# Conv-attention hybrid on one core: tokens' and feed-forward's PSUM banks in one pool, attention's fixed tiles in other memory, an earlier weighted sum, halved totals

## The chip, the cores and the metric

The kernel runs on one core of one Trainium2 chip, in fp32. The metric is the device time of one launch in microseconds (us), the median of several runs. The engines are called by the names that the profile uses: PE is TensorE's matmuls and PEld its weight loads, DVE is VectorE, ACT is ScalarE, POOL is GpSimd, SP starts the transfers. SBUF is the memory on the chip; PSUM holds the results of matmuls, in eight banks of 128 partitions by 512 fp32 elements.

## What is computed

The input has four images of 128 channels and 64 x 64 = 4096 positions. Each goes through a convolutional attention over positions, then, as 4096 tokens of 128, through a self-attention with 16 heads of 8 and a small feed-forward, and last through a recurrence over tokens.

```python
# layer 0, x: [4, 128, 4096]; conv1x1 is W @ x with a prelu
e1, e2, asm = conv1x1(gn(x), w1), conv1x1(gn(x), w2), conv1x1(gn(x), wa)
score = softmax(einsum('nci,ncj->nij', e1, e2), axis=2)      # 4096 x 4096 per image
x = x + einsum('nij,ncj->nci', score, asm)
# layer 1, t: tokens of 128 = 16 heads x 8
q = qz_ring(heads(ln(t)) + rx_theta)                         # products of cosines
attn = softmax(q @ q^T / sqrt(8))                            # queries, keys and values are q
x1 = ln(ln(t) + concat(attn @ q) @ w_comb^T)
h = relu((cos(x1[..., :8]) * cos(ry_theta)) @ w1^T)
t = t + ln(x1 + h @ w2^T)
# last layer: Wx = batchnorm(ln(t) @ W^T), then
y = sigmoid(Wx[:, step] + y @ V)                             # one step after the other
x = from_tokens(t + ys)
```

Since queries and keys are the same q, the scores are symmetric: a tile of exponentials serves once as it is and once transposed.

## The kernel before

**Stages.** A loop over the four images opens, for each, a convolution stage (`first_stage`, L1352) and an attention stage (`second_stage`, L1400). After the last image come its feed-forward alone (`third_stage`) and the recurrence. Each stage has its own pools of SBUF tiles and PSUM banks; they are given as a name with a shape and a number of buffers, and a tile asked for by `get(name, ...)` takes the next buffer of its pool in turn. A tile whose memory was another's before waits for the last reader of the other. The order of the instructions on PE, ACT and DVE is the order in which the program is written (`manual_schedule`); in the attention stage that holds for POOL as well. In time, image 0's convolution stage runs from 24 to 407 us, its attention to 1659, the convolution stage of image 1 to 2118, its attention to 3375, and so on.

**Convolution stage.** For eight blocks of 512 queries (ic) the inner loop goes over sixteen pairs of key tiles (jp), two pairs a turn: `scores` (L503, two matmuls for each of two key tiles, into a PSUM pair), the exponential to SBUF (L507, ACT), and `weigh` (L514, PE) for the pairs of the turn before, which also adds the exponentials on DVE into a `total` of 128 x 2 x 512. `pieces` are the parts of the three 1x1 convolutions of later blocks, put between; the first of them are wanted by the first turns. After each weighted pair `meanwhile` takes one step of this image's `tokens` (generators that stop at each `yield`, L604) and of the *previous* image's `feed_forwards` (L1305, each `feed_forward`, L1119). The tokens of a block: px, the input transposed on PE and copied to SBUF by ACT (L612 to L614); sum, the totals summed over partitions by matmuls with ones (L619 to L630) in four column groups, transposed on DVE (L632) and inverted; pt, the transposed weighted sum (L640); their combination on DVE (L645), normalisation, cosines, and pq, the transposed q (L688), which is written out as the rows that attention's loads read. The eighth group is the tail: the stage runs it to its combination, and the attention stage steps it to its end between its own units.

PSUM in this stage: one bank `ps_acc`, two pairs `ps_pair`, two single banks `ps_one` (feed-forward: pc, pw, pl, pz, ph, pf, pwx and the convolution's pieces) and one `ps_tok` (px, sum, pt, pq, and the norm's small sums).

**Attention stage.** Eight pairs of heads, for each four blocks b of 512 queries x 2 heads; a block has 20, 20, 16 and 16 units, a unit being two key tiles. Written out, a unit is: its scores (L1012, four matmuls into two PSUM pairs of three), their exponentials (L1024, two instructions on ACT, or four if a unit is split: `off` and two different tiles), the weighted sums of the unit two before (L863, four matmuls with the fixed tile q_aug), and some mirror steps (L842): the products with the transposed exponentials, sixteen steps to a group of four units, four matmuls each. An *off* unit hands its exponentials to DVE for the transposing (L829); an *own* unit, whose tiles both lie in the block's own keys, has no such work. How many mirror steps a unit does is set by a credit, and only if a group is due:

```python
rates = (3.3, 3.0) if b < NQB // 2 else (3.15, 3.0)      # off, own
if end_of_all and not off:
    rates = (0, 4.5)
credit = min(credit + rates[0 if off else 1], 4.75)
...
credit -= run_pending(turn, int(credit))
```

`end_of_all` is the last block of an image. A group's last step adds its bank into `later` on DVE (L856).

**Fixed tiles.** `fixed_tiles` (L725) makes q_aug0 and mirror0 at the start, q_aug1 and mirror1 some turns later: POOL fills them (L728, L733), then copies q into them (`prepare`, L745; `mirror_weights`, L799), which the first weighted sums and the first mirror steps wait for. Their place in SBUF follows the order in which the stage's pools are opened (`fixed`, then `exps`), over what the convolution stage left there.

Of the kernel before, what the change touches and what calls it, by code (L numbers as in the profile page):

```python
# [13 lines left out]
ALU = mybir.AluOpType  # L14
# [12 lines left out]
def kernel(  # L27
# [341 lines left out]
    def layer0(n, xs, xh, norm, shifted, begin, meanwhile):  # L369
# [122 lines left out]
        def scores(ic, jp):  # L492

            if shifted and jp == 0:
                halves(ic)
            s = pair_psum(f"s{n}_{ic}_{jp}")
            hl = state["halves", ic].bitcast(F32R)
            for j in range(2):
                parts = [(e2.bitcast(F32R)[:, ts(2 * jp + j, P)], hl[:, y, :]) for y in range(2)]
                if shifted:  # L500
                    parts.append((ones.bitcast(F32R), state["less", ic].bitcast(F32R)))
                for y, (stationary, moving) in enumerate(parts):
                    nc.tensor.matmul(  # L503
                        s[:, j, :], stationary, moving, start=y == 0, stop=y == len(parts) - 1
                    )
            p = mid_tile(f"p{n}_{ic}_{jp}")
            nc.scalar.activation(p, s, AF.Exp)  # L507
            return p
# [36 lines left out]
        for ic in range(NIC):  # L545
            for jp in range(0, NP, 2):
                if jp == NP // 2 and ic < NIC - 1 and not shifted:
                    halves(ic + 1)
                fresh = [(ic, j, scores(ic, j)) for j in (jp, jp + 1)]
                for i in range(2):  # L550
                    if before:
                        weigh(*before[i])
                        if before[i][1] == NP - 1:
                            take(before[i][0])
                            begin(before[i][0], state)
                    if pieces and i == 0:
                        pieces.pop(0)()

                    meanwhile(2 if ic == NIC - 1 else 1)
                before = fresh  # L560
# [43 lines left out]
    def tokens(im, i, sums):  # L604

        n, q, cols = im["n"], im["q"], ts(i, IC)
        last = i == NTG - 1
        yield  # L610

        pt = transposed(blocks(im["xs"][:, cols]), f"px{n}_{i}", "ps_tok")  # L612
        x0 = im["xs"][:, cols] if last else get("thalf", f"x0_{n}_{i}")
        nc.scalar.copy(x0, pt)  # L614
        yield


        total, taken = sums.pop(i), sums.pop(("sum", i))
        ps = get("ps_tok", f"sum{n}_{i}")[:, 0:P]  # L619
        tv = total.rearrange("p j (k c r) -> p j c k r", c=4, r=32)  # L620
        for j in range(2):
            for c in range(4):
                nc.tensor.matmul(
                    ps[ts(c, 32), :],
                    ones[:, 0:32],
                    tv[:, j, c],
                    start=j == 0,
                    stop=j == 1,
                    skip_group_check=True,
                )  # L630
        by_token = once.tile([P, P], F32, tag="sums", name=f"sums{n}_{i}")
        nc.vector.transpose(by_token, ps)  # L632
        if n == "r":
            inv = stats.tile([P, TG], F32, tag="inverse", name=f"inv{n}_{i}")
        else:
            inv = inverses[:, n * NIC + i, :]
        nc.vector.reciprocal(inv, by_token.rearrange("p (k r) -> p k r", k=TG)[:, :, 0])
        if not last:
            yield
        pt = transposed(blocks(taken), f"pt{n}_{i}", "ps_tok")  # L640
        if not last:
            yield
        for k in range(TG):
            at = ts(k, P)
            nc.vector.scalar_tensor_tensor(  # L645
                x0[:, at], pt[:, at], inv[:, k : k + 1], x0[:, at], ALU.mult, ALU.add
            )
        nc.sync.dma_start(out=im["x0"][:, cols], in_=x0)
        yield last
        mv, rstd = token_stats(blocks(x0), TG, 1e-5, f"t{n}_{i}")  # L650
        yield
        yield
        x1 = get("thalf", f"x1_{n}_{i}")
        normalise(blocks(x1), blocks(x0), mv, rstd, TG)
        nc.sync.dma_start(out=im["x1"][:, cols], in_=x1)
        arg, k, r = (get("thalf", f"{name}{n}_{i}") for name in ("arg", "k", "r"))
        nc.vector.tensor_tensor(
            arg.rearrange("p (a d) -> p a d", d=D),
            x1.rearrange("p (a d) -> p a d", d=D),
            rx_bc.unsqueeze(1).broadcast_to([P, IC // D, D]),  # L660
            ALU.add,
        )
        yield
        steps = cos_steps(r, arg, k, r)
        for _ in range(3):
            next(steps)
            yield

        for _ in range(3 if i == NTG - 1 else 0):
            yield  # L670
        next(steps, None)
        yield
        c = r.rearrange("p (a d) -> p a d", d=D)
        qv = q[:, cols].rearrange("p (a d) -> p a d", d=D)
        nc.gpsimd.tensor_tensor(qv[:, :, 0], c[:, :, 1], c[:, :, 2], ALU.mult)
        nc.vector.tensor_tensor(qv[:, :, 1], c[:, :, 0], c[:, :, 1], ALU.mult)
        for d in range(2, D):
            nc.vector.tensor_tensor(qv[:, :, d], qv[:, :, d - 1], c[:, :, d], ALU.mult)
            if d > 2:
                nc.gpsimd.tensor_tensor(qv[:, :, 0], qv[:, :, 0], c[:, :, d], ALU.mult)  # L680
            if d == 4:
                yield
        yield
        yield


        rows = parts_dram.rearrange("(h y d) s -> y h d s", y=2, d=D)
        pt = transposed(blocks(q[:, cols]), f"pq{n}_{i}", "ps_tok")  # L688
        high, low = get("thalf", f"high{n}_{i}"), get("thalf", f"low{n}_{i}")
        pv = pt.rearrange("p (a s c) -> p a s c", a=4, s=4)  # L690
        hv, lv = (t.rearrange("p (s a c) -> p a s c", a=4, s=4) for t in (high, low))
        nc.scalar.copy(hv.bitcast(F32R), pv)
        yield
        nc.vector.tensor_tensor(lv, pv, hv, ALU.subtract)
        for y, part in enumerate((high, low)):
            nc.sync.dma_start(out=rows[y][:, :, cols], in_=part)

    def attention(n, q, xs, tail, upcoming):
# [295 lines left out]
        for pair in range(NPAIR):  # L994
            keys, queries, qa, later, denom = ready
            for b in range(NQB):
# [7 lines left out]
                for at, unit in enumerate(tiles):  # L1004
# [27 lines left out]

                    rates = (3.3, 3.0) if b < NQB // 2 else (3.15, 3.0)
                    if end_of_all and not off:
                        rates = (0, 4.5)
                    credit = min(credit + rates[0 if off else 1], 4.75)

                    if at == 1:
                        credit = max(credit, 3.0)
# [312 lines left out]
    def first_stage(im, before):  # L1352


        n = im["n"]


        ffn = dict(x1=(HALF, 3), fhalf=(HALF, 7), hT=(MID, 2))
        sums = dict(thalf=(HALF, 6), half=(HALF, 2), sums=(MID, 2), hl=(MID, 2))
        rest = dict(e=(BIG, 2), big=(BIG, 1), mid=(MID, 7))  # L1360
        pools = {**ffn, **sums, **rest}
        psum = dict(ps_acc=(ONE, 1), ps_pair=(MID, 2), ps_one=(ONE, 2), ps_tok=(ONE, 1))
        engines = {nc.tensor.engine, nc.scalar.engine, nc.vector.engine}
        others = {"ps_norm": lambda name: get("ps_tok", name)}
        with stage(f"conv{n}", {}, others, **pools, **psum), tc.manual_schedule(engines=engines):
            own, calls = [], [0]
            step_late = in_steps(feed_forwards(before) if before else [], 13, 3)

            def meanwhile(steps=1):

                calls[0] += 1
                if before and calls[0] in (14, 17, 20):
                    before["left"].pop(0)()
                for _ in range(steps):
                    step_first(own)

                for _ in range(0 if calls[0] <= 8 else 2 if calls[0] % 8 == 0 else 1):
                    step_late()

            norm = im["norm"] or list(norm_stats(n, im["xs"]))[-1]  # L1380
            layer0(
                n,
                im["xs"],
                im["q"],
                norm,
                n == "r",
                lambda ic, sums: own.append(tokens(im, ic, sums)),
                meanwhile,
            )
            *own, tail = own  # L1390
            for g in own:
                for _ in g:
                    pass
            while step_late():
                pass
            while not next(tail):
                pass
        return tail

    def second_stage(im, tail, upcoming):  # L1400
# [7 lines left out]
            half=(HALF, 1),  # L1408
            turned=((P, 2 * P), 1),
            other=((P, QT * 2 * D), 1),  # L1410
            fixed=((P,), 1),
            exps=((P, QB), 6),
            flipped=((P, TG, QB), 4),
            ps_acc=(ONE, 1),
            ps_pair=(MID, 3),
# [299 lines left out]
```

## Time and profile before

| | |
|---|---|
| median of 3 runs | 7035.01 us (7033.8 to 7037.29) |
| profiled execution | 7037.54 us, of which the span 7035.8 |
| granted TensorE clock, mean | 0.99 |
| attention, image 0 (407 to 1659) | 1252 us, PE busy 1239.66, ACT 1207.18, DVE 1117.12 |
| convolution stage, image 1 (1659 to 2118) | 459 us, PE busy 442.63, DVE 346.23, ACT 270.78 |
| opening of image 1's attention (2118 to 2160) | 42 us, PE busy 32.14 |
| attention, image 1, after it (2160 to 3375) | 1215 us, PE busy 1209.93, ACT 1175.47 |
| convolution stage, image 2 (3375 to 3835) | 460 us, PE busy 443.64 |
| costliest on PE | mirror steps (L842) 1980 us, weighted sums (L863) 1523 + 942, attention's scores (L1012) 1229 |
| costliest on ACT | attention's exponentials (L1024) 2950 + 1839 us |

A row of the profile with fp32 matmuls counts two passes for each, except where the scores run in one. Rows of groups give how often an instruction ran, its busy time, its mean in ns, and how long its engine sat idle before it. Four fifths of the time are attention, where PE and ACT are both nearly full; most of the time in which PE is idle is in the convolution stages and where attention opens.

### The profile page before, as it was taken

What the parts mean: (1) busy time and instruction counts of PE and PEld (TensorE: products, weight loads), DVE (VectorE), ACT (ScalarE), POOL (GpSimd) and SP (SyncE); (2) the same over time, 40 slices, a digit from 0 to 9 for tenths busy, and PEclk for the clock granted to TensorE, in tenths of its full rate; (3) what the DMA queues carried; (4) which work ended last, traced back from release to release, by engine and by line L of the source; (5) the groups of instructions that cost most, each with busy time, mean ns of one, the idle gap of its engine ahead of it and who ended that gap; (6) DMA issues with size and microseconds to landing.
All of it is one profiled execution on the core that took longest, in us unless ns stands there. A gap on an engine that the chain in (4) does not pass through costs nothing. (4 is left out here: it accounts for less than half of the span.)

```text
span 7035.8 us, 224882 instructions
## 1 busy us (share of the span) xinstructions
PE 6830.7 (97%) x93038; PEld 3709.3 (53%) x93038; DVE 5897.3 (84%) x8054; ACT 5965.7 (85%) x11927; POOL 2760.4 (39%) x9893
## 2 busy tenths in 40 slices
PE   8999999999999999999999999999999999999987
PEld 4545555555654555555565555555466455555546
DVE  6688898987778888888777898888877888889884
ACT  4479999996668999999566999999856699999986
POOL 1134444434333444343433343444443334444431
PEclk9999999999999999999999999999999999999998
DMA  1110000000111000000011100000011100000012
GB/s 31 36 40 25 26 26 21 21 10 25 50 49 37 27 21 22 21 21 22 22 47 49 37 21 21 21 25 22 19 32 44 55 23 21 25 26 25 12 62 109
DMA packets 84797, 220.02 MB, mean 31 GB/s; under 512 B 9400, under 2 KB 10304, under 8 KB 82992
## 3 DMA queue, kind: packets, MB, share of 16 engines
q1 hardware_dynamic: 79584, 194.05, 8.3%
q8 instruction: 731, 11.98, 0.7%
q10 hardware_dynamic: 3888, 11.29, 0.4%
q14 instruction: 306, 2.51, 0.1%
q0 software_dynamic: 288, 0.20, 0.0%
HBM read 141.51 MB, written 56.62 MB: 28 GB/s over the span
## 5 line engine op out<-in xcount | busy, mean ns | idle before, releaser
L1024 ACT ACTIVATE e<-s 128x1024 f32<-128x1024 f32 (+1 forms) x3480 | 2949.9, 901 | 93.0 <-PE s L1012 57.6
L829 DVE STREAM_TRANSPOSE t<-e 128x1024 f32<-128x1024 f32 x2240 | 2587.4, 1208 | 8.9 <-ACT e L1024 6.3
L842 PEld LDWEIGHTS misc<-t,mirror 128*32 128x32 f32 x57344 | 1658.6, 110 | 1367.2 <-issue 1316.4
L842 PE MATMUL misc<-t,mirror 128*32 128x128 f32 x57344 | 1980.1, 273 | 21.3 <-DVE later L856 17.2
L1024 ACT ACTIVATE xs<-s 128x1024 f32<-128x1024 f32 (+1 forms) x2152 | 1839.1, 907 | 58.7 <-PE s L1012 42.5
L829 DVE STREAM_TRANSPOSE t<-xs 128x1024 f32<-128x1024 f32 x1344 | 1558.8, 1208 | 4.7 <-ACT xs L1024 3.2
L863 PE MATMUL acc<-e,q_aug 128*32 128x512 f32 x11360 | 1523.0, 608 | 10.9 <-POOL q_aug L745 10.9
L1012 PE MATMUL s<-queries,keys 32*128 32x512 f32 x9216 | 1229.2, 496 | 8.4 <-ACT e L1024 8.2
L905 POOL COPY own<-o 32x36 f32<-32x36 f32 x2048 | 430.7, 210 | 1803.0 <-DVE o L897 1723.0
L514 PE MATMUL acc<-p,asmT 128*128 128x512 f32 x2048 | 945.5, 593 | 0.0
L863 PE MATMUL acc<-xs,q_aug 128*32 128x512 f32 x7072 | 942.3, 605 | 0.0
L507 ACT ACTIVATE p<-s 128x1024 f32<-128x1024 f32 x512 | 499.8, 1021 | 448.0 <-PE s L503 421.2
L1012 PEld LDWEIGHTS s<-queries,keys 32*128 32x128 f32 x9216 | 485.4, 181 | 535.8 <-issue 326.7
L1024 ACT ACTIVATION_READ_ACCUMULATOR e<-s 128x1 f32 x2880 | 691.6, 240 | 0.0
L930 POOL COPY other<-turned 32x64 f32<-32x64 f32 x1904 | 449.5, 236 | 611.8 <-DVE turned L920 533.3
L799 POOL COPY mirror<-q 32x128 f32<-32x128 f32 x2048 | 594.6, 290 | 199.2 <-PE misc L842 111.2
L503 PE MATMUL s<-hl,e 128*128 128x512 f32 x2048 | 590.1, 429 | 16.4 <-ACT hl L465 8.9
L528 DVE TENSOR_TENSOR total<-total,p 128x1024 f32<-128x1024 f32 x448 | 546.7, 1220 | 28.3 <-ACT p L507 20.2
L514 PEld LDWEIGHTS acc<-p,asmT 128*128 128x128 f32 x2048 | 379.0, 189 | 329.5 <-issue 307.7
L856 DVE TENSOR_TENSOR later<-later,misc 128x128 f32<-128x128 f32 (+1 forms) x576 | 160.1, 278 | 380.6 <-PE misc L842 377.6
L503 PEld LDWEIGHTS s<-hl,e 128*128 128x128 f32 x2048 | 380.3, 189 | 175.1 <-issue 71.7
L890 POOL COPY by_token<-by_key 32x4 f32<-32x4 f32 x2016 | 391.6, 194 | 85.1
(260 smaller groups left out, 4810.0 us busy)
## 6 DMA issues: line engine op xcount, KB each, us to landing
keys<-parts_dram SPq DMA_DIRECT2D x256, 256.0 KB
queries<-parts_dram SPq DMA_DIRECT2D x1024, 32.0 KB
fx<-x_dram SPq DMA_DIRECT2D x64, 256.0 KB
x_dram<-x SPq DMA_DIRECT2D x56, 256.0 KB
xs<-in_x_dram SPq DMA_DIRECT2D x16, 512.0 KB
t_dram<-t2T SPq DMA_DIRECT2D x32, 256.0 KB
t2s<-t_dram SPq DMA_DIRECT2D x16, 512.0 KB
hl<-hl SPq DMA_DIRECT2D x28, 256.0 KB
```

What stands on the lines that cost most here:

```text
L503: nc.tensor.matmul(s[:, j, :], stationary, moving, start=y == 0, stop=y == len(parts) - 1)
L507: nc.scalar.activation(p, s, AF.Exp)
L514: nc.tensor.matmul(state["acc", ic], asmT[:, ts(2 * jp + j, P)], p[:, j, :], start=jp == 0 and j == 0, stop=jp == NP - 1 and j == 1,)
L528: nc.vector.tensor_tensor(state[ic], state[ic], p, ALU.add)
L799: nc.gpsimd.tensor_copy(wv[ts(a, 32), s, :, :, ts(a, D)], own[ts(s, 32)])
L829: nc.vector.transpose(group["e"][h][:, k, :], es[h])
L842: nc.tensor.matmul(state["acc"][ts(2 * x + h, 32), :], state["w"][:, QT * (s // 4) + TG * x + s % 4, h, :], state["e"][h][:, :, ds(IC * x ...
L863: nc.tensor.matmul(it["in"]["acc"][ts(2 * h + x, 32), :], it["qa"][:, ds((2 * it["tiles"][x] + h) * V, 32)], it["e"][h][:, ts(x, IC)], sta ...
L905: nc.gpsimd.tensor_copy(own[ts(s, 32), ts(x, 4), h, :], ov[ts(2 * h + x, 32), s, :, 0:V])
L930: copy(to[ts(k, 32), h], tv[ts(2 * x + h, 32), k])
L1012: nc.tensor.matmul(ss[h][:, x, :], keys[unit[x] // QT].bitcast(F32R)[r, ts(unit[x] % QT, P)], queries[b].bitcast(F32R)[r, :], start=True, ...
L1024: nc.scalar.activation(es[h][:, ts(x, IC)] if split else es[h], ss[h][:, x, :] if split else ss[h].rearrange("p x c -> p (x c)"), AF.Exp, ...
```

## The change

- **One PSUM pool.** In the convolution stage `ps_one` has three banks and `ps_tok` is gone; the tokens' px, sum, pt and pq, and the norm's sums, take their turn in the same pool as the feed-forward's tiles and the convolution's pieces.
- **Other memory for the fixed tiles.** The attention stage opens `exps` before `fixed`, and the convolution stage opens `sums` (the totals) last. So `q_aug` and `mirror` come to lie where exps lay, and the exps over what the convolution stage kept in `thalf`, `half` and `hl`.
- **First weighted sums ahead of the second scores.** At the very first turn of the convolution stage the fresh pairs are put straight into `before`: they are weighted in the same turn, and the second turn's scores come after.
- **Totals halved.** Before the sum over partitions DVE adds the two halves of a total (128x512) at the start of the px step; the sum then takes four matmuls instead of eight.
- **Credits.** An own unit may save up to 8.25 credits where all had 4.75; in the last block of an image the last two own units gain 8.0 instead of 4.5.

```diff
--- before.py
+++ after.py
@@ -547,6 +547,8 @@
                 if jp == NP // 2 and ic < NIC - 1 and not shifted:
                     halves(ic + 1)
                 fresh = [(ic, j, scores(ic, j)) for j in (jp, jp + 1)]
+                if ic == jp == 0:
+                    before, fresh = fresh, []
                 for i in range(2):
                     if before:
                         weigh(*before[i])
@@ -609,25 +611,20 @@
         last = i == NTG - 1
         yield
 
+        total, taken = sums.pop(i), sums.pop(("sum", i))
+        nc.vector.tensor_tensor(total[:, 0, :], total[:, 0, :], total[:, 1, :], ALU.add)
         pt = transposed(blocks(im["xs"][:, cols]), f"px{n}_{i}", "ps_tok")
         x0 = im["xs"][:, cols] if last else get("thalf", f"x0_{n}_{i}")
         nc.scalar.copy(x0, pt)
         yield
 
 
-        total, taken = sums.pop(i), sums.pop(("sum", i))
         ps = get("ps_tok", f"sum{n}_{i}")[:, 0:P]
-        tv = total.rearrange("p j (k c r) -> p j c k r", c=4, r=32)
-        for j in range(2):
-            for c in range(4):
-                nc.tensor.matmul(
-                    ps[ts(c, 32), :],
-                    ones[:, 0:32],
-                    tv[:, j, c],
-                    start=j == 0,
-                    stop=j == 1,
-                    skip_group_check=True,
-                )
+        tv = total[:, 0, :].rearrange("p (k c r) -> p c k r", c=4, r=32)
+        for c in range(4):
+            nc.tensor.matmul(
+                ps[ts(c, 32), :], ones[:, 0:32], tv[:, c], start=True, stop=True
+            )
         by_token = once.tile([P, P], F32, tag="sums", name=f"sums{n}_{i}")
         nc.vector.transpose(by_token, ps)
         if n == "r":
@@ -1032,8 +1029,8 @@
 
                     rates = (3.3, 3.0) if b < NQB // 2 else (3.15, 3.0)
                     if end_of_all and not off:
-                        rates = (0, 4.5)
-                    credit = min(credit + rates[0 if off else 1], 4.75)
+                        rates = (0, 4.5 if at < len(tiles) - 2 else 8.0)
+                    credit = min(credit + rates[0 if off else 1], 4.75 if off else 8.25)
 
                     if at == 1:
                         credit = max(credit, 3.0)
@@ -1356,12 +1353,12 @@
 
 
         ffn = dict(x1=(HALF, 3), fhalf=(HALF, 7), hT=(MID, 2))
-        sums = dict(thalf=(HALF, 6), half=(HALF, 2), sums=(MID, 2), hl=(MID, 2))
-        rest = dict(e=(BIG, 2), big=(BIG, 1), mid=(MID, 7))
-        pools = {**ffn, **sums, **rest}
-        psum = dict(ps_acc=(ONE, 1), ps_pair=(MID, 2), ps_one=(ONE, 2), ps_tok=(ONE, 1))
+        held_late = dict(thalf=(HALF, 6), half=(HALF, 2), hl=(MID, 2))
+        rest = dict(e=(BIG, 2), big=(BIG, 1), mid=(MID, 7), sums=(MID, 2))
+        pools = {**ffn, **held_late, **rest}
+        psum = dict(ps_acc=(ONE, 1), ps_pair=(MID, 2), ps_one=(ONE, 3))
         engines = {nc.tensor.engine, nc.scalar.engine, nc.vector.engine}
-        others = {"ps_norm": lambda name: get("ps_tok", name)}
+        others = {name: one_psum for name in ("ps_norm", "ps_tok")}
         with stage(f"conv{n}", {}, others, **pools, **psum), tc.manual_schedule(engines=engines):
             own, calls = [], [0]
             step_late = in_steps(feed_forwards(before) if before else [], 13, 3)
@@ -1408,8 +1405,8 @@
             half=(HALF, 1),
             turned=((P, 2 * P), 1),
             other=((P, QT * 2 * D), 1),
+            exps=((P, QB), 6),
             fixed=((P,), 1),
-            exps=((P, QB), 6),
             flipped=((P, TG, QB), 4),
             ps_acc=(ONE, 1),
             ps_pair=(MID, 3),
```

## The prediction

> **What bounds the kernel now.** I read the page's first part, then windows by stage, then TensorE's waits, and the timeline where a wait of note sits.
>
> ```profile
> PE 6830.7 (97%) x93038; PEld 3709.3 (53%) x93038; DVE 5897.3 (84%) x8054; ACT 5965.7 (85%) x11927; POOL 2760.4 (39%) x9893
> ...
> 600.00:700.00 100.00, 99.91 (x1732) 50.70 (x1732) 88.13 (x95) 97.44 (x201) 43.29 (x183) 1.00 0.05 15
> ...
> 1900.00:2000.00 100.00, 95.44 (x417) 60.49 (x416) 76.75 (x197) 62.23 (x91) 33.14 (x33) 1.00 0.15 47
> ...
> 2100.00:2200.00 100.00, 90.14 (x1117) 44.11 (x1119) 81.09 (x101) 76.45 (x147) 40.17 (x125) 0.91 0.15 53
> ```
>
> The windows' columns are stretch, length, busy us of PE, PEld, DVE, ACT, POOL, granted clock, DMA share, GB/s. In attention (600:700) TensorE has 0.1 us in 100 free and ScalarE 2.6: two engines side by side, so neither can be held up for long. In the convolution stage with a feed-forward beside it (1900:2000) TensorE lacks 4.6, the others 23 and more: there it loses time to waits, not to work. Where attention opens (2100:2200) it lacks 9.9. So only TensorE's own work and its waits count. The waits:
>
> ```profile
> PE ph L1194 <- ACT last L1316: 20.0, 21, 1.0
> PE misc L842 <- DVE later L856: 17.2, 7, 4.5
> ...
> PE acc L863 <- POOL q_aug L745: 10.9, 2, 5.5
> ...
> PE ph L1194 <- DVE fx L1150: 7.4, 6, 1.3
> ...
> PE s L503 <- ACT z L399: 4.6, 4, 1.3
> ```
>
> (total us, times, longest). Of these the change touches all five.
>
> **What the Trainium skill says.** "TensorE: Matmul & The Clock Gate", Part 3, The mechanism: matmuls start and end in program order, only weight loads are pulled ahead. So one late PSUM bank holds everything behind it; the trace agrees (after each wait above, nothing overtook). Its Part 1 says that TensorE falls to half clock after about 3.4 us of idleness. The trace agrees: after 5.51 us idle the eight rows of L863 (four matmuls) took 1.94 us, elsewhere 1.06. "VectorE: DVE Perf Modes", the section on the TRN2 errata, has (N+151)/0.96 ns for an fp32 add of two tensors: an estimate of 0.69 us for 512 columns; L657, the same shape, measures 0.692.
>
> **1. Totals halved (L615).** One more VectorE add of 128x512 for each of 32 token groups: 32 x 0.69 = 22 us of VectorE, and half of the sum's matmuls are gone: 4 for 8.
>
> ```profile
> L623 PE MATMUL sum<-total,ones 128*32 128x128 f32 x512 | 20.6, 279 | 2.6 <-ACT xs L614 1.6 <-ACT x L614 1.0
> ...
> DVE sums L632 <- PE sum L623: 125.8, 32, 7.5
> ```
>
> 512 rows for 32 groups: 16 each, two passes for each matmul, four column tiles side by side. The mirror step of L842 is the same form, 8 rows, and a unit with one step more is 0.22 us longer (below); so eight rows fewer save 0.22, and 32 x 0.22 = 7.0 us. VectorE waits 125.8/32 = 3.9 us before the transpose that follows, which covers the add. **-7.** If that cover were gone (a busy VectorE at the px step), a group would cost up to 0.69 - 0.22 = 0.5, +15 in all: an end for the range.
>
> **2. One PSUM pool of three banks.** Before, the feed-forward had two banks of its own and the tokens one. In its list of banks, the last ph of a group reuses the bank of pl, transposed 0.4 us before:
>
> ```profile
> 2001.52 0.60 PE L291 MATMUL pl<-ident,q 128*128 128x128 f32 x4
> 2001.87 0.47 PE L1194 MATMUL ph<-zT,f_sb 128*128 128x512 f32 x1
> 2003.29 0.50 PE L1194 MATMUL ph<-zT,f_sb 128*128 128x512 f32 x1 [0.95 <-ACT last L1316]
> ```
>
> It waits for ScalarE to empty pl. There are nine of these in each of images 1 to 3: the 21 waits on last and the 6 on fx of the list, 20.0 + 7.4 = 27.4 us. Further, sum reuses px's bank and pt that of sum: 1.0 (x of L614) and 1.8 us (pt on sums, 2.2 less the 0.44 at one opening). In the changed order of allocation the bank is used again after 1.0 us at the least (ph after sum), 1.2 and 1.7 next, else 2.2 and up. An eviction took 0.6 us and its start some 0.4, so nearly all of the 30 us go. Some will come back where the reader is VectorE, queued behind 1.2-us work. **-25** (between -30 and -18). Nothing else in this stretch is full, so no other engine is late next.
>
> **3. Fixed tiles in memory of exps; px, sum and pt ahead of attention's first scores.** In images 1 and 3 the mirror tile's memory was that of the last taken, so:
>
> ```profile
> 2121.98 1.81 POOL L733 MEMSET mirror<- 128x2048 f32 x1 [18.43 <-PE pt L291]
> 2123.72 5.02 POOL L745 COPY q_aug<-q 32x112 f32<-32x112 f32 x16
> ...
> 2128.80 1.94 PE L863 MATMUL acc<-e,q_aug 128*32 128x512 f32 x8 [5.51 <-POOL q_aug L745]
> ...
> 2152.86 1.93 PE L842 MATMUL misc<-t,mirror 128*32 128x128 f32 x32 [3.57 <-DVE later L856]
> ```
>
> POOL's memset waited 18.4 us for pt, the copies followed, TensorE idled 5.5 us. With the tiles where nothing live ends so late the copies are done long before. But the opening isn't free for that: at 2152.86 TensorE waits again, for VectorE, which was behind with the tail's normalisation and the transposes. What TensorE gains at 2128 it waits for there, except what VectorE itself gains: 1.2 us of waiting on POOL's r_t (POOL no longer busy with copies) and the tail's tokens about 2 us earlier. So -3.3 for images 1 and 3 each instead of -5.5 and more, -1.6 for image 2 (gaps of 1.17 us at its sum and pt, some of the 3.3 at its M), 0 for image 0, whose tiles now wait for the last scores and whose copies end about 2 us after the first weighted sum would like them (+-1). **-8** (between -15 and -2).
>
> **4. First weighted sums ahead of the second scores.** The second pair waited 1.28 us for the convolution's z in a PSUM pair, once per image, 4.6 in all (the list). After the change the third convolution's pair is wanted by scores 0_5 instead, and VectorE's work on it (2.5 us) ends no sooner. **-0.5** (+-2).
>
> **5. The cap on credits, 8.25 for own units.** It reads like a thing for the end of the image, but it decides the steady blocks. A block's units carry (mirror steps; * is an own unit, / one whose exponentials are split in four):
> before, b=2: 2 4 3 *3 3 3 0 *4 3 4 3/ *2 4/ 3/ 3/ *3
> after: 2 4 3 *3 3 3 0 *7 3 3 3/ *0 4/ 3/ 4/ *3.
> The own unit after the 0 takes the saved credit at once, so the group of 16 steps is used up earlier, and the next own unit has none. b=3 is changed alike; b=0 gets b=1's row. The steps are conserved. The trace's law: from scores to next scores is 1.43 us + 0.22 per step (0, 2, 3, 4 steps: 1.43, 1.87, 2.09, 2.31). ScalarE needs 2.04 to 2.08 for an off unit, about 1.9 for an own one, 2.3 for a split one. So a unit without steps is shorter than its exponentials, and the next scores wait for a PSUM pair:
>
> ```profile
> 2691.84 0.50 PE L1012 MATMUL s<-queries,keys 32*128 32x512 f32 x4
> ...
> 2692.39 1.02 ACT L1024 ACTIVATE e<-s 128x1024 f32<-128x1024 f32 x1
> ...
> 2693.28 0.78 PE L1012 MATMUL s<-queries,keys 32*128 32x512 f32 x4
> ...
> 2693.98 1.07 PE L863 MATMUL acc<-e,q_aug 128*32 128x512 f32 x8
> ...
> 2700.78 0.60 ACT L1024 ACTIVATE e<-s 128x512 f32<-128x512 f32 x1 [0.19 <-PE s L1012]
> ...
> 2703.08 1.96 ACT L1024 ACTIVATE e<-s 128x1024 f32<-128x1024 f32 x2
> ```
>
> At 2693.28 the scores last 0.78 instead of 0.51: the weighted sum begins 0.57 us after the exponential ends (2692.39 + 1.02 + 0.57 = 2693.98), 0.27 late. Now the new zero, behind a split unit. The split unit's scores are at S = 2700.25; its four exponentials run from 2700.78 to 2703.08; the own unit's first one ends 1.04 later, S + 3.87, so the weighted sum after comes at S + 4.44. TensorE alone would have it at 2.09 + 1.43 + 0.43 = S + 3.95. That is +0.49 a block. In return the 0.17 at the block's last own unit (31.36 to the next block's 33.62, 2.26 for 2.09), due to the same lag of ScalarE, goes: after the pause the split units have slack. Net +0.32 on 60 blocks (32 of b=2, 28 of b=3; an image's last is another list): +19. b=0: +0.1 x 28 = 3 for its waits at other places, less 2 for their old ones: +1. **+20** (0.1 to 0.57 a block: +6 to +34).
>
> **6. End of an image.** 5, 4, 4 steps in the last units and eight steps ahead of the norm's small matmul instead of one: they fill 0.4 us that TensorE waited for VectorE there. **-1** for three images. For pq, which now shares the pool, **+1**.
>
> **Sum.** -7 - 25 - 8 - 0.5 + 20 - 1 + 1 = -20.5. From the profiled 7037.5 us (span 7035.8 and 1.7 around it): 7017. The median of the runs is 2.5 below the profiled one, so 7014.5, said as **7015**.
>
> **Rivals.** *Attention indifferent*: the zero units cost no more than the lag they take away (0.0 to 0.1 a block); for it, that ScalarE is free 2.6 us in 100 and the 7-step unit lets it catch up; against, the arithmetic of the 0.57. Then 7015 - 17 = 6998. *The pool moves the waits*: three banks for two streams, half of the 25 comes back as waits for VectorE's readers, and the openings give nothing, VectorE setting their end anyway; for it, the 3.57 above; against, reuse distances over 1 us. 7015 + 12 + 7 = 7034. *Slower*: one mechanism, ScalarE's backlog in b=2 and b=3. Behind the new zero come three units (4/ 3/ 4/) of 2.31, 2.09, 2.31 on TensorE against 2.3 on ScalarE; if the lag doesn't run off there, each of them and the last own unit wait again, 0.2 to 0.3 each. The change loses from (20.5 + 20)/60 = 0.68 a block on; at 0.49 + 4 x 0.15 = 1.1 a block the time is 7015 + 60 x (1.1 - 0.32) = 7062. Against it: after a wait TensorE is later, and its own units let ScalarE gain 0.2. *It doesn't do what it says*: banks and tiles that end up waiting for the same things; the built order of allocation shows otherwise; 7030.
>
> **Chances.** Forecast 0.47, attention indifferent 0.28, waits moved 0.15, slower 0.07, nothing done 0.03. What a measurement of this kernel can tell is about 0.2%, 14 us: below 7021 is faster, above 7049 slower. The forecast's own range is 7003 to 7027, three quarters of it below 7021: 0.35; with indifferent 0.28 and 0.02 of the rest, faster 0.65; slower 0.05; same 0.30. The range goes from indifferent with the pool's -30 (6992) to the waits moved (7034).
>
> **What would show it.** The waits of ph on last and fx gone from TensorE's list, its busy share in 1900:2000 at 98; sum at 256 rows; no wait of acc on q_aug at 2128 but a longer one of misc on later; weight loads of scores waiting on e more often, in b=2 and b=3 with the own unit of no steps followed by scores of about 1.0 us. I am wrong if the b=2 and b=3 blocks keep their length (then lower), if they grow by more than 0.7 us each, or if ph keeps waiting.

## The result and the profile after

The changed kernel takes 7007.28 us (median of 6 runs, 7004.61 to 7009.6) where the kernel before, run beside it, takes 7036.59 (6 runs, 7033.8 to 7038.4): ratio 0.9958, 95% interval 0.9946 to 0.9971. It is 29.3 us faster, 0.42%; 7015 was forecast, from steps that sum to -20.5. The profiled execution of the changed kernel took 7005.9 us, its span 7004.2.

The page's first part and three windows of the changed kernel, set at about the same places of the work (columns as before: stretch, length, PE, PEld, DVE, ACT, POOL, clock, DMA share, GB/s). Lines of the changed kernel mostly stand three lower: its L839 is L842 before.

```profile
PE 6828.0 (97%) x92782; PEld 3702.0 (53%) x92782; DVE 5934.9 (85%) x8086; ACT 5960.0 (85%) x11927; POOL 2772.7 (40%) x9893
```

```profile
600.00:700.00 100.00, 99.90 (x1728) 50.57 (x1728) 88.22 (x92) 97.18 (x200) 43.09 (x183) 1.00 0.05 16
1880.00:1980.00 100.00, 99.42 (x428) 64.03 (x427) 79.39 (x205) 64.07 (x92) 33.33 (x37) 1.00 0.15 46
2090.00:2190.00 100.00, 93.10 (x1201) 45.62 (x1203) 85.42 (x106) 81.68 (x169) 44.21 (x120) 0.97 0.16 54
```

The convolution stage, where PE lacked 4.6 us in 100, now lacks 0.6 (2 was forecast). The opening of image 1 lacks 6.9 instead of 9.9. In attention, 600 to 700, the busy share says nothing: PE is full in both, and yet the next section finds it slower there. A wait of a few tenths of a us between matmuls is within the length that the records give to the matmul before it.

TensorE's waits after (line, releaser, total us, times, longest):

```profile
PE misc L839 <- DVE later L853: 17.2, 7, 4.3
PE pg L357 <- DVE gmv L353: 16.1, 1, 16.1
PE s L1009 <- ACT e L1021: 11.4, 18, 1.2
PE s L503 <- ACT hl L465: 11.1, 7, 2.8
PE pq L291 <- DVE q L675: 9.9, 7, 3.2
...
PE s L503 <- ACT p L507: 6.1, 7, 1.1
PE s L1009 <- DMA keys<-parts_dram: 5.9, 1, 5.9
...
PE acc L860 <- POOL q_aug L742: 1.0, 1, 1.0
```

The waits of ph on last (20.0) and on fx (7.4) are gone, that on z (4.6) is gone, and q_aug is down from 10.9 to 1.0. New is one wait of 5.9 us for a transfer of keys, which nothing in the prediction's working foresaw.

To see where the time went I cut both profiled executions at the same matmuls: convolution stage (first L503 to last L514), opening (from there to the start of attention's 21st unit), steady attention (to the start of the image's last block), and the rest up to the next convolution stage. Change in us, all four images:

| | convolution | openings | steady attention | ends | 
|---|---|---|---|---|
| image 0 | -3.5 | +0.4 | +4.2 | +1.2 |
| image 1 | -13.3 | -4.8 | +3.9 | -1.6 |
| image 2 | -13.7 | **+5.5** | +4.0 | -0.2 |
| image 3 | -13.7 | -3.8 | +4.0 | -0.3 |
| sum | -44.2 | -2.6 | +16.1 | -0.9 |

These make -31.6, the difference of the two spans. Where attention isn't touched, its steady stretch repeats within 0.5 us an image from kernel to kernel, mostly within 0.1; the other stretches, where nothing was changed, scatter by about 1.5 us each. Much of that goes with the granted clock. Where no part of an image's end ran at half clock, that end took 52.7 to 52.9 us in every kernel (images 0 to 2); where 3.41 us or more did, it took 54.1 to 54.5 in 11 cases of 17.

### The profile page after: what moved, and what is told of

Its sections match the earlier page's. It is cut to its first block, busy times and chain, and to the rows that moved or that the text cites. A ratio compares the mean times of both kernels' runs of the same rounds, so it can differ in the third digit from the quotient of the medians.

```text
span 7004.2 us, 224421 instructions
## 1 busy us (share of the span) xinstructions
PE 6828.0 (97%) x92782; PEld 3702.0 (53%) x92782; DVE 5934.9 (85%) x8086; ACT 5960.0 (85%) x11927; POOL 2772.7 (40%) x9893
## 5 line engine op out<-in xcount | busy, mean ns | idle before, releaser
L839 PEld LDWEIGHTS misc<-t,mirror 128*32 128x32 f32 x57344 | 1656.9, 110 | 1329.6 <-issue 1271.7
L839 PE MATMUL misc<-t,mirror 128*32 128x128 f32 x57344 | 1968.9, 273 | 20.1 <-DVE later L853 17.2
L1009 PE MATMUL s<-queries,keys 32*128 32x512 f32 x9216 | 1246.6, 496 | 19.3 <-ACT e L1021 11.4
L514 PE MATMUL acc<-p,asmT 128*128 128x512 f32 x2048 | 945.5, 593 | 1.8 <-DVE e L410 1.6
L507 ACT ACTIVATE p<-s 128x1024 f32<-128x1024 f32 x512 | 499.6, 1023 | 416.8 <-PE s L503 368.9
L503 PE MATMUL s<-hl,e 128*128 128x512 f32 x2048 | 587.9, 428 | 17.9 <-ACT hl L465 11.1
L514 PEld LDWEIGHTS acc<-p,asmT 128*128 128x128 f32 x2048 | 379.6, 190 | 334.5 <-issue 309.4
L503 PEld LDWEIGHTS s<-hl,e 128*128 128x128 f32 x2048 | 380.8, 189 | 172.7 <-issue 69.5
L1021 ACT ACTIVATION_READ_ACCUMULATOR xs<-s 128x1 f32 x1728 | 422.0, 244 | 0.0
```

The costliest lines, as they stand in the source:

```text
L503: nc.tensor.matmul(s[:, j, :], stationary, moving, start=y == 0, stop=y == len(parts) - 1)
L514: nc.tensor.matmul(state["acc", ic], asmT[:, ts(2 * jp + j, P)], p[:, j, :], start=jp == 0 and j == 0, stop=jp == NP - 1 and j == 1,)
L839: nc.tensor.matmul(state["acc"][ts(2 * x + h, 32), :], state["w"][:, QT * (s // 4) + TG * x + s % 4, h, :], state["e"][h][:, :, ds(IC * x ...
L1009: nc.tensor.matmul(ss[h][:, x, :], keys[unit[x] // QT].bitcast(F32R)[r, ts(unit[x] % QT, P)], queries[b].bitcast(F32R)[r, :], start=True, ...
L1021: nc.scalar.activation(es[h][:, ts(x, IC)] if split else es[h], ss[h][:, x, :] if split else ss[h].rearrange("p x c -> p (x c)"), AF.Exp, ...
```

## The experiments

Each kernel's difference is to the kernel before, run beside it. Where it is smaller than the interval of the ratio, the stage lengths carry the verdict.

**The pool of banks alone** (on the kernel before):

```diff
-        psum = dict(ps_acc=(ONE, 1), ps_pair=(MID, 2), ps_one=(ONE, 2), ps_tok=(ONE, 1))
+        psum = dict(ps_acc=(ONE, 1), ps_pair=(MID, 2), ps_one=(ONE, 3))
-        others = {"ps_norm": lambda name: get("ps_tok", name)}
+        others = {name: one_psum for name in ("ps_norm", "ps_tok")}
```

> The kernel before with the one PSUM pool of three banks alone. Theory now (waits of less than a matmul's modelled tail are hidden in the busy time, so there was more to win than the list of waits showed): 32 to 35 us shorter than before, each of the three later convolution stages by 11. Rival (the recorded prediction's term): 25, and the rest of what the convolution stages gained belongs to the halved totals and the earlier weighted sums. Rival 2: the pool moves the waits, 12 or less.

6998.4 against 7036.69: ratio 0.9946 (0.9929 to 0.9962), -38.3 us. The three later convolution stages are 12.7, 11.8 and 11.9 shorter, image 0's (no feed-forward) is as it was, and the openings are 5.5 shorter together. That is more than the theory gave, and far from both rivals: this one edit gains more than the whole change.

**Only pl elsewhere** (two pools as before; the transposed pl goes into the tokens' bank):

```diff
-        pt = transposed(blocks(u), f"pl{n}_{i}")
+        pt = transposed(blocks(u), f"pl{n}_{i}", "ps_tok" if n in range(N - 1) else "ps_one")
```

> The kernel before with its two pools, and only pl (in the convolution stages) taken from the tokens' bank instead of the feed-forward's two. Theory (the distance of reuse is what matters, ph after pl after 0.4 us, not the number of banks in one pool): ph's waits on last go, 27 to 30 us shorter, 7010 beside 7038; the sums' and pt's waits and the openings stay as they were, so it falls 8 to 11 short of the pool alone. Rival (one bank for five kinds of tokens' tiles stalls instead): 15 us or less.

7012.5 against 7035.49: 0.9967 (0.9954 to 0.9979), -23.0. The timeline at the same place of image 1:

```profile
1998.12 0.60 PE L291 MATMUL pl<-ident,q 128*128 128x128 f32 x4
1998.47 0.71 PE L1194 MATMUL ph<-zT,f_sb 128*128 128x512 f32 x2
1999.02 1.98 PE L503 MATMUL s<-hl,e 128*128 128x512 f32 x8
```

Both ph of the pair run together, 1.42 us from the first to the second before. Its wait list has no ph on last; the six on fx stayed (7.4), and so did those of sum (1.6) and pt (2.2) and the openings (-0.2). So it is the distance of reuse. The 23.0 are less than the 27 to 30 expected, whose lower end is ph's two waits together (20.0 and 7.4), and fx's part stayed; pl itself now waits 1.3 for sums. Summed over the convolution stages of images 1 to 3, the intervals from the start of the matmul before to each ph are 55.0 us in the kernel before, 31.6 here, 25.4 in the pool alone: 23.3 for pl, 6.3 more for the pairs that waited on fx. The list of waits had 20.0 for the 21, the intervals show 23.3: 0.16 us of each wait was booked as busy time of the matmul before. The rest of the pool's 38.3 lies elsewhere: sum, px and the transposes called pt (of tokens and of the feed-forward) come 6.5 us sooner in the convolution stages, less 3.9 of longer waits of pq and pw, and the openings are 5.5 shorter. These make 37.7. The two traces differ by 41.2 (6996.35 and 7037.54); the rest is spread over the scores, the weighted sums and pc, and is no more than what untouched stretches scatter by.

**The pool undone** (the changed kernel with two pools):

> The changed kernel with two pools again (ps_one of two banks, ps_tok of one). Theory (the parts hardly touch each other): it stands to before as the sum of the other parts measured alone, -7.6 + 0.6 - 0.1 + 14.1 = +7 us, so about 7044, and the waits of ph on last are back at 20 us and 21 times. Rival (pool and tiles share the openings: either one lets POOL's copies end in time): the pool is worth 5 us less here than alone, about 7040.

7042.0 against 7035.49: 1.0010 (1.0003 to 1.0016), +6.5. The other parts alone sum to +7.0, so the parts add up; the wait of ph on last is back with the very 20.0 us in 21 waits. The rival holds in part all the same: in the traces' openings the pool is worth 2.4 us inside the change and 5.5 alone. The time can't tell the two apart. Without the pool the change would make the kernel slower.

**Halved totals alone:**

```diff
+        nc.vector.tensor_tensor(total[:, 0, :], total[:, 0, :], total[:, 1, :], ALU.add)
...
-        tv = total.rearrange("p j (k c r) -> p j c k r", c=4, r=32)
-        for j in range(2):
-            for c in range(4):
+        tv = total[:, 0, :].rearrange("p (k c r) -> p c k r", c=4, r=32)
+        for c in range(4):
...
```

> The kernel before with the totals halved alone. Theory: 0.22 us for each of 32 sums, of which seven lie in each convolution stage (1.5 us a stage) and one in each opening: 7 us shorter, 7030 beside 7036.7, VectorE's 22 us hidden in its wait before L632. Rival (VectorE's add delays what is queued behind it): no gain or up to 8 us longer.

7030.63 against 7038.2: 0.9990 (0.9983 to 0.9997), -7.6. In the changed kernel a sum takes 0.356 us to the next matmul, before 0.574: 0.218 less each, 32 x 0.218 = 7.0. In the groups of the changed kernel the row has half the count. That it has no wait is the pool's doing: with the halving alone the 2.6 us of before stay. VectorE's adds, 21.9 us in all, lie in the wait ahead of the transpose: it shrank from 125.8 to 104.6 us with the halving alone, and to 97.8 in the changed kernel:

```profile
L625 PE MATMUL sum<-total,ones 128*32 128x128 f32 x256 | 13.6, 285 | 0.0
```

```profile
DVE sums L629 <- PE sum L625: 97.8, 32, 7.2
```

**First weighted sums alone:**

```diff
                 fresh = [(ic, j, scores(ic, j)) for j in (jp, jp + 1)]
+                if ic == jp == 0:
+                    before, fresh = fresh, []
```

> The kernel before with the first weighted sums ahead of the second scores alone. Theory (the wait for z is only moved to the scores two turns on): the convolution stages change by less than 1 us each, the time by less than 3 us. Rival (it is a part of what the convolution stages won beyond the pool): 2 us a stage, 8 in all.

7038.82 against 7038.2: 1.0001 (0.9993 to 1.0010). No difference that can be told. The 4.6 us on z are gone, and in their place the list has 6.0 us on p (L507), 1.5 before, in waits of up to 1.1; the changed kernel has 6.1.

**Credits alone:**

```diff
-                    credit = min(credit + rates[0 if off else 1], 4.75)
+                    credit = min(credit + rates[0 if off else 1], 4.75 if off else 8.25)
-                        rates = (0, 4.5)
+                        rates = (0, 4.5 if at < len(tiles) - 2 else 8.0)
```

> The kernel before with the credits alone (cap 8.25 for own units, 8.0 for the last two). Theory (the steps' distribution alone decides, not tiles or banks): 16 us longer, 4.0 in each image's steady attention, b=2 blocks 0.45 and b=3 blocks 0.25 longer; the ends of images gain 1 at most: 7052 beside 7036.7. Rival (it needs the rest of the change to cost anything): under 5 us.

7052.28 against 7038.2: 1.0019 (1.0012 to 1.0026), +14.1; steady attention 4.3 to 4.4 longer in every image. So tiles and banks have no part in it.

**The cap undone** (the changed kernel, 8.25 only in an image's last block):

```diff
-                    credit = min(credit + rates[0 if off else 1], 4.75 if off else 8.25)
+                    credit = min(credit + rates[0 if off else 1], 8.25 if end_of_all and not off else 4.75)
```

> The changed kernel with the own units' cap back at 4.75 except in an image's last block. Theory (the zero-step own unit behind a split one costs, net of what it takes away): the steady blocks get their old lengths, 16 us shorter in all: 6991 beside 7007, and in b=2 and b=3 the scores of 4/ last 2.31 from start to start instead of 2.71. Rival (attention indifferent, the longer blocks in the changed trace come from elsewhere, such as tiles in other memory): no difference, 7007 within 3.

6991.18, 16.1 below the changed kernel's 7007.28; against before (7036.69) 0.9935 (0.9918 to 0.9952). Steady attention is back to its old length within 0.05 us an image. The rival is out.

The timeline of a b=2 block in the changed kernel (image 1, pair 3) shows the price:

```profile
2688.39 0.51 PE L1009 MATMUL s<-queries,keys 32*128 32x512 f32 x4
2688.82 1.07 PE L860 MATMUL acc<-e,q_aug 128*32 128x512 f32 x8
2689.82 0.90 PE L1009 MATMUL s<-queries,keys 32*128 32x512 f32 x4
2690.65 1.07 PE L860 MATMUL acc<-e,q_aug 128*32 128x512 f32 x8
2691.53 1.06 PE L839 MATMUL misc<-t,mirror 128*32 128x128 f32 x32
2692.52 0.51 PE L1009 MATMUL s<-queries,keys 32*128 32x512 f32 x4
```

```profile
2687.42 0.59 ACT L1021 ACTIVATE e<-s 128x512 f32<-128x512 f32 x1
...
2689.13 1.96 ACT L1021 ACTIVATE e<-s 128x1024 f32<-128x1024 f32 x2
```

The own unit at 2688.39 has no mirror step; the next scores, at 2689.82, last 0.90, and their weighted sum comes 0.83 after their start instead of 0.43: 0.40 late. ScalarE came to the own unit's exponentials only at 2689.13, after the split unit's four. From these scores to the next are 2.70 us, 2.31 by the law that the prediction read from the kernel before (four steps).

**The SBUF part alone** (exps ahead of fixed in attention, totals last in the convolution stage):

```diff
-        sums = dict(thalf=(HALF, 6), half=(HALF, 2), sums=(MID, 2), hl=(MID, 2))
-        rest = dict(e=(BIG, 2), big=(BIG, 1), mid=(MID, 7))
+        held_late = dict(thalf=(HALF, 6), half=(HALF, 2), hl=(MID, 2))
+        rest = dict(e=(BIG, 2), big=(BIG, 1), mid=(MID, 7), sums=(MID, 2))
...
-            fixed=((P,), 1),
             exps=((P, QB), 6),
+            fixed=((P,), 1),
```

> The kernel before with the SBUF part alone: exps opened ahead of fixed in attention, the totals last in the convolution stage. Theory: the openings of images 1 and 3 lose the 5.5 us wait for q_aug and get back some 2 to 3 us as a longer wait for later, so -2.5 to -3.5 each; image 2's opening is 4 to 6 us longer through the key tile over the last total; image 0's 0 to 2 longer: in all between -2 and +3 us. Rival (the recorded term): 8 us shorter, image 2 among them with 1.6.

7038.1 against 7038.2: 1.0000 (0.9991 to 1.0009). Openings by image: -0.6, -3.8, **+6.2**, -2.6. Images 1 and 3 gain what the theory says, and image 2 gives it back. Its wait list, first SP's own and then PE's:

```profile
SPq L768 <- PE sum L623: 5.9, 1, 5.9
```

```profile
PE s L1012 <- DMA keys<-parts_dram: 5.3, 1, 5.3
```

In images 0 and 2 the keys lie at the other end of SBUF. Image 0's first loads go out at 272 us, long before its attention opens at 407, and don't wait. In image 2 the first key tile came to lie where the last total is, whose reader is the tail's sum, at the very end of the stage. SP, which issues in order, holds the loads until then. In the changed kernel's timeline of that opening:

```profile
3808.89 0.43 PE L625 MATMUL sum<-total,ones 128*32 128x128 f32 x8
...
3809.38 1.14 SPq L765 DMA_DIRECT2D keys<-parts_dram  x2
...
3811.63 2.19 SPq L765 DMA_DIRECT2D keys<-parts_dram  x4
3815.82 0.79 PE L1009 MATMUL s<-queries,keys 32*128 32x512 f32 x2 [5.91 <-DMA keys<-parts_dram]
```

**The keys freed** (the changed kernel, the totals' pool ahead of mid, so that image 2's first key tile comes to lie over another tile):

```diff
-        rest = dict(e=(BIG, 2), big=(BIG, 1), mid=(MID, 7), sums=(MID, 2))
+        rest = dict(e=(BIG, 2), big=(BIG, 1), sums=(MID, 2), mid=(MID, 7))
```

> The changed kernel with the totals' pool opened ahead of mid instead of after it; only image 2's first key tile gets another neighbour (p instead of total). Theory (the 5.9 us wait for keys at image 2's opening is the key tile lying over the last total, whose reader is the sum): the wait is gone, the first scores of image 2 come 0.2 to 1.2 us after the px step as in the other images, and the time is 5 to 7 us shorter. Rival (the queue of SP is late anyway, or VectorE sets the opening's end as in images 1 and 3): the wait for keys goes, the one for later grows by as much, under 2 us in all.

6999.64, 7.6 below the changed kernel; to before 0.9946 (0.9929 to 0.9962). Image 2's first scores:

```profile
3808.49 0.73 PE L1009 MATMUL s<-queries,keys 32*128 32x512 f32 x6
```

1.9 us after the start of the stage's last weighted-sum matmul, as in the other images, for 7.88 in the changed kernel. Its opening is 3.5 shorter than the changed kernel's in the profiled executions, and 7.1 in the kernel with both edits (below). The wait for later doesn't explain the difference: it is 3.5 us in that opening of the changed kernel, none here and 1.3 with both edits. What does go with it is a longer wait of scores for e (5.0 us here, 3.5 with both) and the granted clock: 20.5 us of this opening ran at half clock here, 13.7 with both. Which of them leads is not shown.

**Both** (the cap undone and the keys freed):

> The changed kernel with both: the cap back at 4.75 except in the last block, and the totals ahead of mid. If both are costs that only happen to come with the change and don't touch each other, 16 + 6 = 22 us below it, 6985. If they share a limit (VectorE in the openings), 16 to 18.

6984.19: 0.9926 (0.9909 to 0.9942) to before, -52.5 us, and 23.1 below the changed kernel. The two costs add. It is the fastest kernel of the study.

## Why the prediction came out as it did

The direction and the time were right, by parts that were off on both sides. That the forecast came within 8 us is partly luck: the pool gave 14 more than its term and the credits cost 5 less, and the tiles gave 8 less.

| step | recorded | measured |
|---|---|---|
| 1 halved totals | -7 | -7.6 |
| 2 pool (and pq, +1) | -24 | -38.3 |
| 3 fixed tiles, order of the opening | -8 | -0.1 |
| 4 first weighted sums | -0.5 | +0.6 |
| 5, 6 credits, end of an image | +19 | +14.1 |
| sum | -20.5 | -31.3 alone; -29.3 together |

Step 1 held in size, in place and in its cover (VectorE's add lies in its wait at L632).

Step 2 was right in mechanism, reuse of pl's bank after 0.4 us, which the run that moves pl alone shows by itself. The size was off by 14. The term took 5 of the listed 30 off for waits that would come back through VectorE; only pq and pw gave some back (3.9). It took the list at its word, where the intervals from start to start had 29.6 for ph instead of 27.4. And the openings' part, 5.5, was booked in step 3: that px, sum and pt run without waits between them is the pool's doing. In the pool alone pt starts 1.53 us after the start of the stage's last matmul, in the SBUF part alone 2.84, as in image 0 before. POOL's memset of the mirror tile waits for that pt, so in images 1 and 3 the wait for q_aug is 2.8 us with the pool alone, where it was 5.5 and 5.4.

Step 3 failed as a sum. Its central argument held: q_aug's 5.5 us vanish, and part comes back; -3.3 an image was recorded, -3.8 and -2.6 measured. What comes back isn't all at the wait for later, where the prediction put it (3.57 to 4.35 in image 1 of the changed kernel, but 3.8 to 3.2 in image 3). With the SBUF part alone, image 1's matmuls have gained 7.0 us three units on: 5.5 for the wait and 1.5 because the units behind it no longer run at half clock (eight rows of L863 take 1.07 us instead of 1.94). Of that some 1.7 goes at the first mirror steps, which come to wait for POOL's r_t and for t, VectorE's transposes, and 1.1 at later. But the step looked at what fixed tiles and exps come to lie over, and not at what the totals, moved last, come to lie under. Image 2, put at -1.6, was +6.2. The keys' transfers don't occur in its working.

Step 4 held in size: the wait is handed on. It went to the exponentials' p (4.5 us more there), and not, as recorded, to VectorE's work on the third convolution, for which scores wait 0.4 us.

Step 5 held in its reading of the code and in the block where it bites: b=2 blocks grow by 0.45 us and b=3 by 0.24 (28 to 32 blocks of each, scatter 0.03 at most), b=0 shrink by 0.20, b=1 stay. Two sizes were off. One mirror step of each pair goes from b=0 (65 steps to 64) to b=2 (47 to 48), so the text's "the steps are conserved" is true for a pair, not for a block: 0.22 of b=2's 0.45 and of b=0's 0.20 is only that. The net of the pause is 0.23 where 0.32 was recorded, since the new zero costs 0.40, not 0.49. The 0.57 us from the end of an exponential to the weighted sum was read at an off unit, whose exponential is followed by the read of the accumulator, 0.09 later; an own unit has none, and there 0.48 pass (2690.17 to 2690.65). The rival of a lasting backlog fell: the units after the pause have their old lengths, and the 0.17 at the block's end goes as recorded. That attention doesn't care fell as well, by two runs.

Step 6 is too small to be told from the sum: the ends changed by -0.9 in all, with a scatter of 1.5 each. In image 2, whose end ran at full clock in both traces, it is 0.20 shorter, and 0.17 with the credits alone, where -0.3 an image was recorded.

## What to carry to other kernels

A ring of PSUM banks is sized by the shortest distance between two uses of one bank, and the waits for it are worth more than the list says; look at start-to-start intervals of the instructions concerned, and find the one tile that closes the ring too soon. When the order of pools is changed, list for every tile of the next stage what it now lies over, transfers' targets first: one neighbour cost image 2's opening as much as the move gained elsewhere. A limit that is meant for the end of a loop but stands in the loop's body decides the steady blocks: print the schedule it makes before and after.

## What was not expected of the hardware

A wait between two matmuls shorter than the recorded length of the first doesn't appear as idle time: 21 waits of 0.95 us in the list were worth 23.3 us, 1.11 each. In steady attention the changed kernel takes 4 us more in each image, with PE's busy share at 99.9% in both. And the release of a PSUM pair after an exponential with a running sum comes 0.09 us later than after one without (0.57 and 0.48 us from its end to the weighted sum behind it; medians of 148 and 65 such waits in the changed kernel). At 60 places in the kernel that is 5.4 us, more than the 5.0 that this kernel's six runs span.
